# Two heads to a product in the weighted values, and the second layer in one block

## The chip, the cores and the metric

The kernel runs on one core of a Trainium2 chip. A core has five engines that run their own instruction streams: TensorE (PE; its weight loads are listed apart as PEld), VectorE (DVE), ScalarE (ACT), GpSimd (POOL) and SyncE (SP), which issues most transfers. They are kept in order by semaphores. Matmul results land in PSUM, from which DVE and ACT read them. The metric is the device time of one execution in microseconds, the median of several runs. Everything is float32.

## The reference

Two layers on an image batch of 16 x 192 channels x 56 x 56. The first is a shifted-window attention block with six heads of 32 channels and windows of 7 x 7 = 49 positions; the second scales a masked 3 x 3 depthwise convolution by weights made from the image's own mean. Cut to what matters (`_ln` normalises over channels; the roll by 3 and the split into windows are left in words):

```python
h = roll(_ln(x), -3); win = windows_of_7x7(h)            # (-1, 49, 192)
q, k, v = split_heads(win @ qkv_w + qkv_b)                # 6 heads of 32
attn = softmax((q * SCALE) @ k.T + rel_bias + mask)
out = (attn @ v) @ proj_w + proj_b
x1 = x + roll(windows_back(out), 3)
y = gelu(_ln(x1) @ fc1_w + fc1_b) @ fc2_w + fc2_b
x2 = x1 + y
# second layer: weights from the image's mean, then four causal taps
t = relu(bn(mean(x2) @ w1.T)); wt = (t @ w2.T + b2) * mask
out = depthwise_conv3x3(x2, wt) + bias
```

## The kernel before

The work is cut into 64 strips (`S = 16 * NU`, NU = 4). A strip is seven rows of the image's upper half and seven of its lower half; the halves lie in partitions 0 to 63 and 64 to 127 (index `ab`), channels in three groups of 64 (`g`). So a strip holds 2 x 8 windows of 49 positions, `UT = 392` columns for each half.

A software pipeline runs over rounds `r` (the loop at L1349): round r computes the scores of strip r, the weighted values and the projection of strip r-1, the first layer (192 to 768 channels, six chunks `f`) of strip r-2 and the second layer (768 to 192) of strip r-3, and queries, keys and normalisation of strips ahead. Rounds 3 to 63 are full ones.

Nothing is issued straight away. `add(engine, duration, fn, reads, writes)` enters an operation into a plan with the author's estimate of its duration; `Plan.order()` (L72) then lists all of it. TensorE keeps the order in which its operations were added. The other engines take, among operations that are ready soonest, the one that is due first. The resulting list is one program: each engine executes its instructions strictly in that order, waiting on semaphores where the framework finds that two instructions touch the same data.

PSUM is four buffers `ps0` to `ps3` of 128 x 2 x 512 numbers, taken in turn by `bank()` (L186). A buffer has two halves, `p[:, 0]` and `p[:, 1]`, with a key of their own in the plan.

The steps that matter:

- `queries_keys` (L465): three products; q goes by ACT to `q128` and `q2` as one run of 392 columns (with 16 columns of padding), k by DVE and ACT to block tables `kbd`, `kbd2` (L492, L514, L523).
- `scores` (L533): 3 x 16 products, each 64 queries (49 and the 15 columns after them) against the keys of two heads, 98 columns. Then for each of three buffers on DVE the position bias is added (L574) and the maximum taken (L584), POOL subtracts it (L589), ACT exponentiates (L596), DVE sums and inverts (L601, L602), POOL scales (L607).
- `turn_shares` (L611): DVE transposes the shares in blocks of 32 x 32 (L618), and ten transfers on SP (L624) bring them to `pt` with keys in the partitions, queries in two blocks of 32 and 17.
- `values` (L642): v of strip r, into `v0` or `v1` by ACT (L665).
- `weighted` (L672): 4 window pairs x 2 halves x 6 heads x 2 windows = 96 products, each 32 channels of one head by 64 query columns (L690). Four ACT copies (L714) bring the result to `o1` (four heads) and `o2` (two heads), stored with the seven window rows outermost.
- `projection` (L717): `narrow` for o2 (L726), then `broad` for o1 (L740); DVE adds the result to the strip (L764).
- `first_layer` (L770): products (L777) and the ACT gelu into `hid` (L789). `second_layer` (L795): for each g, six steps f of two products (L816), then DVE adds the result to the strip (L803). Each g takes a PSUM buffer of its own, of which it uses half 0.
- `deviations` and `spread` (L306, L347): TensorE folds sums over channels (L316), ACT and DVE make the variance `m2` (L330, L337), ACT makes 1/sqrt with Ln and Exp (L352, L359), and transfers spread it over the partitions as `rb`.
- `taps` and `conv` (L831, L886): the second layer of the network, on TensorE for one small product per image (L846), then ACT and DVE, which apply four taps (L907, L931).

`second_layer` and `weighted` are generators before. The round lets them alternate on TensorE: three steps f after the scores, then one window pair and two steps f in turn, three more steps, then v, the projection, and the last six steps. The first layer is split after two chunks to let `deviations` in.

Of the kernel before, what the change touches and what calls it, by code (L numbers as in the profile page):

```python
# [33 lines left out]
TL = 32  # L34

# [105 lines left out]
def tile_swin_then_dynamic_conv(  # L141
# [64 lines left out]
    q128 = sb("q128", 128, 2, UP)  # L206
    q2 = sb("q2", 128, UP)
# [6 lines left out]
    o1 = sb("o1", 128, WS, 2, NWIN, WS)  # L214
    o2 = sb("o2", 128, WS, 2, NWIN // 2, WS)
# [17 lines left out]
    bnr = sb("bnr", 128, 4, RED)  # L233
# [14 lines left out]
    full = sb("full", 128, 128)  # L248
    eps_t = sb("eps", 128, 1)
    zero = sb("zero", 128, IMG)  # L250
    ident = sb("ident", 64, 64)
# [54 lines left out]
    def deviations(norms, later=False):  # L306
# [36 lines left out]
        if later:  # L343
            return
        spread(norms)

    def spread(norms):  # L347
        lanes = slice(64 * norms[0], 64 * norms[-1] + 64)
# [32 lines left out]
    def first_deviations():  # L381
# [9 lines left out]
        add("PE", 1.4, product, [("f", 0, 0), ("f", 0, 1), "blk"], [pk])  # L391
# [73 lines left out]
    def queries_keys(s, parts):  # L465
        d = xs1
        for i in parts:
# [15 lines left out]
            if i == 0:  # L483
                def go(p=p):
                    nc.scalar.activation(
                        q128[:, :, 0:UT], p[:, :, 0:UT], AF.Identity, bias=qbs[:, 0:1], scale=SCALE
                    )
                add("ACT", 0.95, go, [pk, "qb"], ["q128"])
# [12 lines left out]
            else:  # L501
                for ab in range(2):
                    def go(p=p, ab=ab):
                        nc.scalar.activation(
                            q2[P(ab), 0:UT],
                            p[0:64, ab, 0:UT],
                            AF.Identity,
                            bias=qbs[0:64, 1:2],
                            scale=SCALE,
                        )  # L510
                    add("ACT", 0.62, go, [pk, "qb"], [("q2", ab)])
# [21 lines left out]
    def scores(s):  # L533

        last = s % NU == NU - 1
        for j in range(3):
            p, pk = bank()

            def product(j=j, p=p):
                for w in range(NWIN):  # L540
                    for i in range(2):
                        cols = slice(w * N, w * N + 64)
                        if j < 2:
                            a, k = q128[P(i), j, cols], kbd[P(i), j, w]
                        else:
                            a, k = q2[P(i), cols], kbd2[P(i), w]
# [3 lines left out]
                            a,  # L550
# [6 lines left out]
            if j < 2:  # L557
                keys = ["q128", ("kbd", 0), ("kbd", 1), "qpad"]
            else:
                keys = [("q2", 0), ("q2", 1), "qpad"]  # L560
                keys += [("kbd2", ab, h) for ab in range(2) for h in range(2)]
# [110 lines left out]
    def weighted(s):  # L672


        pa, ka = bank()
        pb, kb = bank()

        def product(pair):
            for ab in range(2):
                for h in range(HEADS):  # L680
                    for w in range(2):
                        if h < 4:
                            j, slot = ab, (h // 2) * 8 + pair * 2 + h % 2
                            at = (ab * 4 + pair) * 64
                            lane, p = TL * h, pa
                        else:
                            j, slot = 2, ab * 8 + pair * 2 + h - 4
                            at = (ab * 2 + pair % 2) * 64
                            lane, p = TL * (h - 4) + 64 * (pair // 2), pb
                        nc.tensor.matmul(  # L690
                            p[lane : lane + TL, w, at : at + 64],
                            v[s % 2][P(w), ab, pair, h * HD : (h + 1) * HD],
                            pt[P(w), :, 16 * j + slot, :],
# [5 lines left out]
        for pair in range(4):  # L699
            add(  # L700
                "PE",
                0.75,
                lambda pair=pair: product(pair),
                PTK() + [("v", s % 2, pair // 2), "ptz"],
                [ka, kb],
            )
            yield
        o1v = o1.rearrange("p r a (q w) c -> p w (a q) r c", w=2)
        o2v = o2.rearrange("p r a (q w) c -> p w (a q) r c", w=2)
        for o, p, k, n, dur in ((o1v, pa, ka, 8, 0.54), (o2v, pb, kb, 4, 0.37)):  # L710
            for w in range(2):
                def go(o=o, p=p, n=n, w=w):
                    src = p[:, w, 0 : 64 * n].rearrange("p (q t) -> p q t", t=64)[:, :, 0:N]
                    nc.scalar.copy(o[:, w], src.rearrange("p q (r c) -> p q r c", c=WS))  # L714
                add("ACT", dur, go, [k], [("o", n, w)])

    def projection(s):  # L717
        pf, kf = bank()
        pq, kq = bank()
        keys = [("o", n, w) for n in (4, 8) for w in range(2)]  # L720

        def narrow():
            for m in range(G):
                for ab in range(2):
                    for i, p in ((0, pf), (1, pq)):
# [3 lines left out]
                            o2[P(i), :, ab],  # L729
                            start=(m % 2 == 0),  # L730
                            stop=False,
# [4 lines left out]
        def broad():  # L736
            for i, p in ((0, pf), (1, pq)):
                for m in range(G):
                    for ab in range(2):
# [3 lines left out]
                            o1[:, :, ab, 4 * i : 4 * i + 4],  # L743
                            start=False,
                            stop=True,
# [4 lines left out]
        add("PE", 1.05, narrow, keys + ["wp"], [kf, kq])  # L750
        add("PE", 2.0, broad, keys + ["wp"], [kf, kq])
# [18 lines left out]
    def first_layer(s, chunks):  # L770
        for f in chunks:
# [23 lines left out]
    def second_layer(s):  # L795

        b, u = divmod(s, NU)
        xv = rows(s).rearrange("p g r c -> p g (r c)")
        for g in range(G):
# [205 lines left out]
    def masks():  # L1005
# [5 lines left out]
        def go():  # L1011
            nc.gpsimd.memset(q128[:, :, UT:UP], 0.0)
            nc.gpsimd.memset(q2[:, UT:UP], 0.0)
# [510 lines left out]
```

## Time and profile before

| what | value |
|---|---|
| median of 3 runs | 2927.38 us (2925.48 to 2928.41) |
| the profiled execution | 2926.42 us, span 2924.6 us, mean granted TensorE clock 0.988 |
| busy, share of the span | PE 97%, DVE 60%, POOL 56%, ACT 48% |
| TensorE groups, busy | L816 837.8, L777 786.5, L473 404.9, L653 266.3, L690 190.4, L548 147.0 us |
| one steady round (scores to scores, 1647.80 to 1691.47) | 43.67 us, TensorE busy 43.67, clock 1.00 |

Busy times of groups on one engine can overlap at their ends, since matmuls are pipelined; the distance from the start of one block to the start of the next is what a block costs. In a timeline line the first number is the start, the second the length, both in us, then engine, line, operation, output and input, and the number of instructions merged. Each float32 product is two instructions. What stands in brackets is idle time before and what ended it. A share of busy time says nothing of what a wait costs; for that one looks at what TensorE waits for.

### The profile page before, as it was taken

The numbers are of one execution on the slowest core, as the hardware profiler recorded it, in microseconds if no ns is written. First come the engines' busy times: TensorE is split into PE (matmuls) and PEld (weight loads), VectorE is DVE, ScalarE is ACT, GpSimd is POOL, SyncE is SP. The second block draws the span as 40 slices with busy tenths as digits, with TensorE's granted clock in tenths as the row PEclk, the third lists the DMA queues.
The fourth block names the chain that finished last, engine by engine and source line by source line (L and its number), as shares of the span: only waits on it lengthen the run. The fifth ranks groups of instructions, "written<-read, shape, count | busy, mean of one in ns | idle before, by whom it ended". The sixth has DMA issues, their size and how long they took to land.

```text
span 2924.6 us, 90872 instructions
## 1 busy us (share of the span) xinstructions
PE 2849.4 (97%) x40401; PEld 1702.8 (58%) x40401; DVE 1758.0 (60%) x2873; ACT 1407.2 (48%) x1890; POOL 1641.6 (56%) x1424
## 2 busy tenths in 40 slices
PE   6799999999999999999999999999999999999996
PEld 4565565565565565565565565565655555565552
DVE  4644664846657475674846657575674846657554
ACT  2344454545445454454545455454454555455443
POOL 4554664755656565664755656565664755656530
PEclk8899999999999999999999999999999999999998
DMA  3511141323314223141322414223141322413221
GB/s 88 109 43 41 42 109 34 82 60 67 87 31 95 59 60 76 42 105 38 82 60 66 88 31 94 59 60 76 42 104 39 81 61 66 88 31 73 47 46 48
DMA packets 123715, 190.84 MB, mean 65 GB/s; under 512 B 31693, under 2 KB 98106, under 8 KB 123322
## 3 DMA queue, kind: packets, MB, share of 16 engines
q1 hardware_dynamic: 118954, 185.01, 28.7%
q8 instruction: 317, 5.19, 0.7%
q10 hardware_dynamic: 4368, 0.02, 0.1%
q14 instruction: 76, 0.62, 0.1%
HBM read 67.57 MB, written 38.93 MB: 36 GB/s over the span
## 4 chain that ended last, share of the span: by engine, by line
PE 95%; DVE 1%; POOL 1%; issue 1%; ACT 1%; DMA 0%; ACTq 0%; DVEq 0%; SPq 0%; POOLq 0%
PE ps L816 28%; PE ps L777 26%; PE ps L473 13%; PE ps L653 8%; PE ps L690 6%; PE ps L740 5%; PE ps L548 5%; PE ps L726 2%; PE ps L316 2%; DVE hid L931 0%; PE ps L846 0%; POOL xs L429 0%; DMA wqkv<-in_L_conv_qkv_w_dram 0%; DVE bt L1250 0%; POOL fold L302 0%
## 5 line engine op out<-in xcount | busy, mean ns | idle before, releaser
L816 PE MATMUL ps<-hid,wf 128*64 128x392 f32 x4608 | 837.8, 499 | 0.3 <-issue 0.3
L777 PE MATMUL ps<-xs,wf 64*128 64x392 f32 x4608 | 786.5, 492 | 0.0
L589 POOL TENSOR_TENSOR e<-e,top 128x784 f32<-128x784 f32 x192 | 314.1, 1659 | 603.0 <-DVE top L584 603.0
L777 PEld LDWEIGHTS ps<-xs,wf 64*128 64x128 f32 x4608 | 440.4, 187 | 315.8 <-issue 16.2
L816 PEld LDWEIGHTS ps<-hid,wf 128*64 128x64 f32 x4608 | 303.5, 136 | 323.2 <-issue 289.6
L789 ACT ACTIVATE hid<-ps,b1f 128x784 f32<-128x784 f32 x384 | 345.8, 913 | 259.3 <-PE ps L777 254.7
L931 DVE SCALAR_TENSOR_TENSOR y<-x,wt,y 128x770 f32<-128x770 f32 x270 | 389.5, 1453 | 64.7 <-ACT y L907 61.0
L473 PE MATMUL ps<-xs,wqkv 64*128 64x392 f32 x2304 | 404.9, 503 | 19.0 <-POOL xs L440 19.0
L607 POOL TENSOR_TENSOR e<-e,tot 128x784 f32<-128x784 f32 x192 | 316.8, 1664 | 43.3 <-DVE tot L602 27.4
L473 PEld LDWEIGHTS ps<-xs,wqkv 64*128 64x128 f32 x2304 | 221.5, 190 | 201.2 <-POOL xs L440 29.8
L293 ACT ACTIVATE sq<-x 128x1176 f32<-128x1176 f32 x128 | 151.4, 1183 | 327.8 <-DVE x L764 235.5
L574 DVE TENSOR_TENSOR e<-ps,bt 128x784 f32<-128x784 f32 x192 | 175.0, 967 | 218.9 <-ACT hid L789 218.8
L300 POOL TENSOR_TENSOR fold<-sq 128x392 f32<-128x392 f32 x128 | 130.7, 1021 | 304.4 <-PE ps L316 268.5
L653 PE MATMUL ps<-wqkv,xs 64*64 64x192 f32 x6144 | 266.3, 326 | 0.0
L653 PEld LDWEIGHTS ps<-wqkv,xs 64*64 64x64 f32 x6144 | 231.0, 134 | 50.7 <-issue 36.1
L596 ACT ACTIVATE e<-e 128x784 f32<-128x784 f32 x192 | 165.2, 861 | 193.7 <-POOL e L589 193.4
L803 DVE SCALAR_TENSOR_TENSOR x<-ps,vecs,x 128x392 f32<-128x392 f32 x192 | 119.8, 624 | 227.1 <-PE ps L816 216.2
L429 POOL TENSOR_TENSOR xs<-x,rb 128x343 f32<-128x343 f32 x192 | 216.3, 1154 | 64.0 <-PE ps L653 61.5
L618 DVE STREAM_TRANSPOSE tt<-e 128x512 f32<-128x512 f32 x384 | 247.9, 687 | 3.4 <-POOL e L607 1.8
L690 PEld LDWEIGHTS ps<-pt,v 64*32 64x32 f32 x12288 | 149.7, 105 | 154.3 <-issue 117.0
L300 POOL TENSOR_TENSOR fold<-x 128x392 f32<-128x392 f32 x128 | 151.4, 1183 | 156.4 <-PE ps L316 124.4
L492 DVE TENSOR_SCALAR kbd<-ps,bq,mask 128x784 f32<-128x784 f32 x128 | 134.1, 1089 | 167.1 <-PE ps L473 167.1
(104 smaller groups left out, 3068.6 us busy)
## 6 DMA issues: line engine op xcount, KB each, us to landing
pt<-tt SPq DMA_DIRECT2D x256, 192.0 KB
x<-in_x_dram SPq DMA_DIRECT2D x112, 294.0 KB
out_dram<-y SPq DMA_DIRECT2D x135, 196.0 KB
pt<-tt SPq DMA_DIRECT2D x256, 96.0 KB
rb<-rsd SPq DMA_DIRECT2D x118, 196.0 KB
out_dram<-y SPq DMA_DIRECT2D x45, 154.0 KB
x<-in_x_dram SPq DMA_DIRECT2D x16, 168.0 KB
pt<-tt SPq DMA_DIRECT2D x128, 12.0 KB
```

Of the source, the lines that this page charges most:

```text
L300: nc.gpsimd.tensor_tensor(f, src[:, 0], src[:, 1], ALU.add)
L429: nc.gpsimd.tensor_tensor(d[:, g, 0 : nf * N].rearrange("p (w r c) -> p w r c", r=WS, c=WS), xv[:, g, :, cs].rearrange("p r (w c) -> p w r ...
L473: nc.tensor.matmul(p[:, ab, 0:UT], lhs_qk(ab, g, i), d[P(ab), g, 0:UT], start=(g == 0), stop=(g == G - 1), tile_position=(64 * ab, 0),)
L589: nc.gpsimd.tensor_tensor(ev, ev, top[j].broadcast_to([128, 16, N]), ALU.subtract)
L607: nc.gpsimd.tensor_tensor(ev, ev, tot[j].broadcast_to([128, 16, N]), ALU.mult)
L618: nc.vector.transpose(tt[:, kb, 16 * j : 16 * j + 16], src)
L653: nc.tensor.matmul(p[P(w % 2), ab, i * DIM : (i + 1) * DIM], d[P(ab), g, w * N : w * N + 64], wqkv[P(ab), g, 2 * DIM :], start=(g == 0), s ...
L690: nc.tensor.matmul(p[lane : lane + TL, w, at : at + 64], v[s % 2][P(w), ab, pair, h * HD : (h + 1) * HD], pt[P(w), :, 16 * j + slot, :], s ...
L777: nc.tensor.matmul(p[:, ab, 0:UT], wf1[P(ab), g, f * 128 : (f + 1) * 128], xs2[P(ab), g], start=(g == 0), stop=(g == G - 1), tile_position ...
L789: nc.scalar.activation(hid[:, f], p[:, :, 0:UT], AF.Gelu, bias=b1f[:, f : f + 1])
L816: nc.tensor.matmul(p[P(ab), 0, 0:UT], wf2[:, f, g * 64 : (g + 1) * 64], hid[:, f, ab], start=(f == 0), stop=(f == NFC - 1), tile_position= ...
L931: nc.vector.scalar_tensor_tensor(dst, s_, w[:, g, t : t + 1], dst, ALU.mult, ALU.add)
```

## The change

Line numbers shift by a few. What changes:

- Weighted values: two heads share a product. 64 channels (two heads of v) meet the shares of both heads, in 2 heads x 2 blocks x 25 columns = 100 columns; the blocks of head 0 with head 0 and head 1 with head 1 are what is wanted, the others are not read. 48 products in three PSUM buffers instead of 96 in two. Twelve copies of 32 partitions, six on ACT and six on DVE, take out the wanted blocks, instead of four on ACT.
- For that the 49 queries are stored as 25 and 24 in two blocks of 32, from q onwards: q is written in two parts, bias and mask tables follow suit (with four more transfers at the start). `o1` and `o2` are stored by window with 49 in a row, and the projection reads them in row order. `broad` comes before `narrow`.
- Order on TensorE in a full round: scores, v, weighted values, second layer whole, projection, q and k, first layer whole, deviations. Before: scores, second layer and weighted values in turns, v, projection, rest of the second layer, q and k, first layer with deviations inside.
- The second layer takes two PSUM buffers: g = 0 and 1 in the halves of one, g = 2 in the other.
- Tables that are used only at the start (`full`, `ident`, `bnr`) share space with `hid`.

```diff
-    q128 = sb("q128", 128, 2, UP)
-    q2 = sb("q2", 128, UP)
+    q128 = sb("q128", 128, 2, NWIN, 2, TL)
+    q2 = sb("q2", 128, NWIN, 2, TL)
...
-    o1 = sb("o1", 128, WS, 2, NWIN, WS)
-    o2 = sb("o2", 128, WS, 2, NWIN // 2, WS)
+    o1 = sb("o1", 128, 2, NWIN, N)
+    o2 = sb("o2", 128, 2, NWIN // 2, N)
...
             if i == 0:
-                def go(p=p):
-                    nc.scalar.activation(
-                        q128[:, :, 0:UT], p[:, :, 0:UT], AF.Identity, bias=qbs[:, 0:1], scale=SCALE
-                    )
-                add("ACT", 0.95, go, [pk, "qb"], ["q128"])
+                for h, lo, hi in ((0, 0, QL), (1, QL, N)):
+                    def go(p=p, h=h, lo=lo, hi=hi):
+                        nc.scalar.activation(
+                            q128[:, :, :, h, 0 : hi - lo],
+                            p[:, :, 0:UT].rearrange("p a (w t) -> p a w t", t=N)[:, :, :, lo:hi],
...
+                    add("ACT", 0.6, go, [pk, "qb", "qpad"], [("q128", h)])
...
     def weighted(s):
-        pa, ka = bank()
-        pb, kb = bank()
-        def product(pair):
-            for ab in range(2):
-                for h in range(HEADS):
+        banks = [bank() for _ in range(3)]
+        def product(j):
+            p = banks[j][0]
+            for t in range(4):
+                for h in range(2):
                     for w in range(2):
...
+                        shares = pt[P(w), :, slot : slot + 2, 0:QL]
                         nc.tensor.matmul(
-                            p[lane : lane + TL, w, at : at + 64],
-                            v[s % 2][P(w), ab, pair, h * HD : (h + 1) * HD],
-                            pt[P(w), :, 16 * j + slot, :],
+                            p[lane : lane + 64, w, t * 128 : t * 128 + 4 * QL],
+                            v[s % 2][P(w), ab, pair, head * HD : (head + 2) * HD],
+                            shares.rearrange("p q k c -> p k q c"),
...
+            for i in range(4):
+                lanes = slice(TL * i, TL * i + TL)
+                at = (i % 2) * 2 * QL
+                src = p[lanes].rearrange("p w (t c) -> p w t c", c=128)[:, :, :, at : at + N]
...
+                if i < 2:
+                    add("ACT", 0.6, lambda dst=dst, src=src: nc.scalar.copy(dst, src), [k], [("o", j, i)])
+                else:
+                    add("DVE", 0.56, lambda dst=dst, src=src: nc.vector.tensor_copy(dst, src), [k], [("o", j, i)])
...
-                            o1[:, :, ab, 4 * i : 4 * i + 4],
+                            o1[:, ab, 4 * i : 4 * i + 4].rearrange(by_rows, c=WS),
...
-        add("PE", 1.05, narrow, keys + ["wp"], [kf, kq])
-        add("PE", 2.0, broad, keys + ["wp"], [kf, kq])
+        add("PE", 2.05, broad, o1k + ["wp"], [kf, kq])
+        add("PE", 1.05, narrow, o2k + ["wp"], [kf, kq])
...
     def second_layer(s):
+        pairs = [bank(), bank()]
         for g in range(G):
-            p, pk = bank()
+            p, pk = pairs[g // 2][0][:, g % 2], pairs[g // 2][1][g % 2]
...
-            nc.gpsimd.memset(q128[:, :, UT:UP], 0.0)
-            nc.gpsimd.memset(q2[:, UT:UP], 0.0)
+            nc.gpsimd.memset(q128, 0.0)
+            nc.gpsimd.memset(q2, 0.0)
...
+        if has(r):
+            values(r, (0, 1))
+        if has(r + 1) and r > -2:
+            scaled1(r + 1)
...
-        for n in (2, 2, 2):
-            next(weighing, None)
-            few(n)
-        for _ in weighing:
-            pass
-        few(3)
+        if has(r - 1):
+            weighted(r - 1)
         if has(r):
             turn_shares()
+        if has(r - 3):
+            second_layer(r - 3)
...
             table("gelu_and_others")
-            first_layer(r - 2, (0, 1))
-            if norms:
-                deviations(norms, True)
-            first_layer(r - 2, range(2, NFC))
+            first_layer(r - 2)
             table("natural_log_exp_and_others")
-            if norms:
-                spread(norms)
-        elif norms and r > -2:
+        if norms and r > -2:
             deviations(norms)
```

## The prediction

> **What bounds the kernel now.** I read the page first: busy shares, then the chain that ended last.
>
> ```profile
> span 2924.6 us, 90872 instructions
> ...
> PE 2849.4 (97%) x40401; PEld 1702.8 (58%) x40401; DVE 1758.0 (60%) x2873; ACT 1407.2 (48%) x1890; POOL 1641.6 (56%) x1424
> ...
> PE 95%; DVE 1%; POOL 1%; issue 1%; ACT 1%; DMA 0%; ACTq 0%; DVEq 0%; SPq 0%; POOLq 0%
> ```
>
> TensorE is the path. TensorE's waits add up to some 47 us, nearly all in the first 130 us, so every microsecond of matmul time counts, and so does every new wait. Next, the timeline of TensorE over one steady round (scores to scores, 1647.80 to 1691.47, 43.67 us) and at the end of the run:
>
> ```profile
> 1647.80 2.25 PE L548 MATMUL ps<-kbd,q 64*64 64x98 f32 x96
> 1649.98 2.20 PE L816 MATMUL ps<-hid,wf 128*64 128x392 f32 x12
> 1652.11 0.72 PE L690 MATMUL ps<-pt,v 64*32 64x64 f32 x48
> 1652.76 1.54 PE L816 MATMUL ps<-hid,wf 128*64 128x392 f32 x8
> 1654.23 0.73 PE L690 MATMUL ps<-pt,v 64*32 64x64 f32 x48
> ...
> 1661.35 4.13 PE L653 MATMUL ps<-wqkv,xs 64*64 64x192 f32 x96
> 1665.30 1.18 PE L726 MATMUL ps<-o,wp 64*64 64x196 f32 x24
> ...
> 1668.45 4.12 PE L816 MATMUL ps<-hid,wf 128*64 128x392 f32 x24
> 1672.50 6.20 PE L473 MATMUL ps<-xs,wqkv 64*128 64x392 f32 x36
> ...
> 1682.57 0.87 PE L316 MATMUL ps<-fold,blk 128*32 128x196 f32 x16
> ```
>
> ```profile
> 2858.64 12.07 PE L816 MATMUL ps<-hid,wf 128*64 128x392 f32 x72
> 2870.64 12.12 PE L777 MATMUL ps<-xs,wf 64*128 64x392 f32 x72
> 2882.70 12.07 PE L816 MATMUL ps<-hid,wf 128*64 128x392 f32 x72
> ```
>
> I take a block's cost from start to next start. The reader is to see that the second layer (L816) is cut in six, and what it costs whole: 12.00 us.
>
> Last, the views of who waits for whom between the engines that read PSUM (ACT and DVE groups, and their timeline):
>
> ```profile
> 1546.92 0.68 ACT L514 ACTIVATE kbd<-ps,km,mask 64x392 f32<-64x392 f32 x1 [3.04 <-PE ps L473]
> ...
> 1547.64 1.30 DVE L523 TENSOR_SCALAR kbd<-ps,bq,mask 64x392 f32<-64x392 f32 x2 [0.59 <-ACT kbd L514]
> 1548.98 0.68 ACT L514 ACTIVATE kbd<-ps,km,mask 64x392 f32<-64x392 f32 x1 [1.37 <-DVE kbd L523]
> ```
>
> ACT reads half 0 of one PSUM buffer, DVE half 1, and still they take turns, with 0.04 us between: the program orders accesses by whole buffers of two halves. This carries the prediction.
>
> **What TensorE gains, per round.**
> - Second layer: its six blocks take 2.13+1.47+1.47+1.46+2.13+4.05 = 12.71 us; whole 12.00. Gain 0.71.
> - Weighted values: four visits of 0.65+0.66+0.70+0.70 = 2.71 us. After: 48 products of 64 by 64 with 100 columns, one block. The scores are the same thing with 98 columns (48 products, 2.18 us), so 2.18 x 100/98 = 2.22. Gain 0.49. Bounds: the rate of the v block (3.95 us for 192 columns) gives 2.06; adding 0.12 for a cut (12 records of L816 take 2.13 against 2.00 pro rata) gives 2.34. I stay with the scores, the nearest shape.
> - First layer uncut: 4.04+0.80+8.10 becomes 12.06+0.80. Gain 0.08.
> - Scores, v, projection and q/k keep their products (2.18, 3.95, 3.15, 6.03). The projection now reads o in runs of 7 numbers where it had 28; no row has such short runs. Bounds: 0 to a doubling of its 3.15 us; I take 0, as the runs of 32 in L690 kept up with 14 ns per record.
>
> New round without waits: 2.18+3.95+2.22+12.00+3.15+6.03+12.06+0.80 = 42.39, a gain of 1.28 us; 61 full rounds (r = 3 to 63): 78 us.
>
> A rule speaks against the weighted values. The Trainium skill, "TensorEngine Tiling (Array Packing)", Available Configurations: the array is 8 tiles at 64x32, 4 at 64x64. By it and the scores' rate (12 x 98 column steps in 2.18 us, 1.85 ns each), 12 x 64 steps cost 1.42 us now and 12 x 100 cost 2.22: a loss of 0.8 us a round, 49 us in all, where the trace's 2.71 gives a gain of 30. The trace decides.
>
> **What the change makes TensorE wait for.** Three pieces, read from the code and the instruction order of the changed program.
>
> (a) The second layer puts g=0 and g=1 in the two halves of one buffer. The changed program lets the third step (f=2) of g=1 wait for the DVE addition that ends g=0 (L803 before), which itself waits for steps f=0,1 of g=1. In every round this is a full turn TensorE-DVE-TensorE. Before, each g had its own buffer and L816 shows no such wait.
>
> (b) In DVE's queue that addition stands behind: three score additions, three maxima, six copies of weighted values, and the first sum of exponentials with its reciprocal. Before, there were no copies on DVE.
>
> (c) The copies of one buffer alternate DVE, ACT, DVE, ACT, each waiting for the one before, as L514/L523 do. ACT's three exponentials stand behind its six copies, and the first sum waits for the first of them.
>
> Clock from the start of the scores: DVE's additions start at 1.04 (1648.84 in the trace), last 2.66, maxima 2.71: free at 6.41 (6.77 with the m2 subtraction of 0.36 between). First weighted buffer: 2.18+3.95+0.74 = 6.87, and a reader starts 0.28 later (v: 1663.60 against 1663.32): 7.15. The copies: 6 on DVE and 4 on ACT lie in series (the last ACT copy of a buffer runs beside the next buffer's first DVE copy). ACT has a row, 392 elements from PSUM: 523 ns. DVE has none: 566 ns (L402, same size) is nearest; 409 ns (196 elements, L764) and 696 ns (L523) bound it. 6 x 0.56 + 4 x 0.52 + 8 x 0.04 = 5.76: until 12.91. First exponential 0.86+0.04: 13.81. Sum and reciprocal 0.04+0.94+0.25: 15.04. Addition 0.63: 15.67; TensorE goes on at 15.72 (0.05 after DVE, as at 2895.80).
> TensorE is ready for f=2 of g=1 at 2.18+3.95+2.22 + 16/36 x 12.00 = 13.68. **Wait: 2.04 us**, more than the 1.28 gained: 0.76 lost, x 61 = 46 us.
>
> Bounds of this wait: if DVE is on time, 0.21 (2894.91 against 2894.70) + 0.63 + 0.05 = 0.9; with 696 and 583 ns (L504) per copy the series is 6.8 and the wait 3.1. DVE's sums, transposes and additions behind it shift with TensorE, and nothing else is due earlier.
>
> The Trainium skill, "PSUM — Partial Sum Buffer", PSUM bank collisions, says that two engines may work at once on different banks, or in different 32-partition quadrants of one. By it neither (a) nor (c) need wait, and the sum would be 2926.4 - 78 + 13 = 2861. The rows of L514 and L523 show the program waiting nevertheless, and it is the program that runs.
>
> **The other edits.**
> - deviations after the first layer: the subtraction m2 (0.36) on DVE stands after the first score addition in the rounds with convolutions: 1.04+0.89+0.36+0.05 = 2.34, and v needs its buffer at 2.18. Wait 0.16 x 45 rounds = 7 us (0 to 0.5 each). rs leaves about 0.35 later, for a q/k product 20 us off: hidden.
> - q written in two blocks: ACT 2 x about 0.5 for 0.91, 4 x about 0.37 for 2 x 0.58: +0.4 us on ACT, 48% busy. First layer's fourth buffer needs them; in the walk they end 0.8 us ahead. Zero; if that cover went, at most 0.4 x 61 = 24.
> - Convolutions (1.45 each, four between g=1 and the projection's additions) end before q/k's third buffer, because TensorE comes 2 us later; without the wait of (a) they would cost about 0.6 in 45 rounds.
> - pt transfers: transposes end some 7 us before the next scores, ten issues take 7.4 us (1664.57), and the weighted values start 6.1 into the round against 4.3 before. Hidden.
> - Start: POOL's zeroing of q, 1536 elements at the 2.66 us of 3072, about 1.3 us, fits in its 2.27 us wait for x. Four more SP issues delay what follows them by 4 x 0.65 us; the bias tables on DVE start at 39.6, long after. kbd2 is now ahead of the tables (the 5.48 us wait goes; the next wait, on xs, shrinks by about 3). In r = 1 and 2 no second layer hides the copies: 5.76 in series plus two sums where 1.37 stood, about +7. Net +4 (-3 to +8).
> - End: two whole second layers with the turn of 0.9 each: +2.
>
> Sum against the profiled execution, 2926.42 us (span 2924.6 and 1.8 around it): +46 +7 +4 +2 = 2985.4; the median of the runs, 2927.38, lies 1.0 higher: **2986**.
>
> **Rivals.**
> 1. Faster: DVE reaches the addition nearly on time. One mechanism: the copies' series. If it takes under 4.8 us in place of 5.76, the wait of (a) is under 1.07 and the kernel wins (1.28 less the 13 us of the other edits over 61 rounds). For it: they touch 32 partitions and contiguous rows of 49. Against: L714 shows 365 ns for 196 elements and 523 for 392, so size along a partition sets it. At the floor of 0.9: 2926.4 - 0.38 x 61 + 13 = 2916, 2917 on the median. Chance 0.17, waits up to 1.16 counted in.
> 2. The turn of (a) costs nothing and the gain stands: 2927 - 78 + 13 = 2862. Against it: the wait is in the program, with 0.9 as its least price. 0.03.
> 3. Copies as slow as the upper rows: 3.1 per round, 2987 + 1.1 x 61 = 3053. For it: L523 on DVE. 0.08.
> 4. Short runs slow the projection: doubled, 2986 + 3.15 x 61 = 3178. 0.03.
>
> **Numbers.** The likeliest case (0.69) is a wait of 1.5 to 2.8: net 0.2 to 1.5 lost per round, with the 13 of the other edits 2953 to 3032, and 2986 in it. Reaching under the floor of rival 1, by the 2.06 us that the weighted values may take (0.16 x 61 = 10), and into rival 3: 2906 to 3040. Within 0.2% (5.9 us; less can't be told from no change in this kernel) means a wait of about 0.97 to 1.16 us: 0.07 of rival 1. Faster: its other 0.10 and 0.03 of rival 2. Slower: 0.69 + 0.08 + 0.03 = 0.80.
>
> **What would show it.** L816's line (L821 after) with a wait on DVE (L808) in nearly every round, some 2 us each, 100 to 130 us in all; otherwise dense TensorE. Weighted values as one block of 96 records in 2.2 us, the second layer in 12.0 plus the wait. DVE copies with ACT as releaser and ACT copies with DVE as releaser. Wrong if the wait is near 0.9, if the copies overlap, or if the projection's block leaves 3.15.

## The result, and the profile after

The changed kernel takes 3001.45 us (median of 4 runs, 2999.95 to 3006.45) against 2927.51 (4 runs, 2925.48 to 2928.41): 1.0257 times as long, 95% interval 1.0239 to 1.0274. The profiled execution took 2999.95 us, span 2998.2, granted clock 0.987 (0.988 before). The forecast was 2986 in 2906 to 3040, slower.

The page of the changed kernel, busy time by engine and the chain that ended last:

```profile
PE 2798.4 (93%) x34257; PEld 1713.7 (57%) x34257; DVE 1924.7 (64%) x3257; ACT 1510.7 (50%) x2210; POOL 1626.8 (54%) x1424
...
PE 75%; DVE 14%; ACT 6%; issue 3%; POOL 1%; DMA 0%; DVEq 0%; ACTq 0%; POOLq 0%
PE ps L782 25%; PE ps L821 15%; PE ps L468 13%; PE ps L653 8%; DVE o L718 7%; PE ps L745 5%; ACT o L716 3%; PE ps L731 3%; DVE tot L601 2%; PE ps L548 2%; ACT e L596 2%; PE ps L689 2%; PE ps L317 2%; DVE x L808 1%; DVE m L338 1%
```

TensorE works 51 us less than before and the kernel takes 73.6 us more of span. The chain, 95% TensorE before, now runs through DVE and ACT: copies (L718, L716), exponentials (L596), sums (L601), the addition (L808). What TensorE waits for (waits by releaser: total us, times, longest):

```profile
PE ps L821 <- DVE x L808: 110.9, 64, 2.3
PE ps L468 <- POOL xs L435: 17.7, 4, 6.3
PE ps L548 <- DVE m L338: 11.7, 15, 0.8
PE ps L745 <- ACT q L505: 11.3, 2, 5.8
```

One wait carries it: the second layer, on DVE's addition, once in every round. Here is a steady round on TensorE, 44.65 us where it was 43.67:

```profile
1643.94 2.25 PE L548 MATMUL ps<-kbd,q 64*64 64x98 f32 x96
1646.28 4.13 PE L653 MATMUL ps<-wqkv,xs 64*64 64x192 f32 x96
1650.23 2.24 PE L689 MATMUL ps<-pt,v 64*64 64x100 f32 x96
1652.40 5.49 PE L821 MATMUL ps<-hid,wf 128*64 128x392 f32 x32
1659.67 6.80 PE L821 MATMUL ps<-hid,wf 128*64 128x392 f32 x40 [1.79 <-DVE x L808]
1666.31 2.34 PE L745 MATMUL ps<-o,wp 128*64 128x196 f32 x24
1668.57 1.31 PE L731 MATMUL ps<-o,wp 64*64 64x196 f32 x24
1669.81 6.20 PE L468 MATMUL ps<-xs,wqkv 64*128 64x392 f32 x36
```

The second layer breaks off after 32 records: 24 of g = 0 and the first two steps of g = 1. And the same stretch on DVE:

```profile
1651.16 0.56 DVE L718 COPY o<-ps 32x392 f32<-32x392 f32 x1 [0.55 <-PE ps L689]
1652.27 1.17 DVE L718 COPY o<-ps 32x392 f32<-32x392 f32 x2 [0.55 <-ACT o L716]
1653.98 1.17 DVE L718 COPY o<-ps 32x392 f32<-32x392 f32 x2 [0.54 <-ACT o L716]
1655.69 0.57 DVE L718 COPY o<-ps 32x392 f32<-32x392 f32 x1 [0.55 <-ACT o L716]
1657.69 0.97 DVE L601 TENSOR_REDUCE tot<-e 128x16 f32<-128x784 f32 x1 [1.43 <-ACT e L596]
1658.70 0.25 DVE L602 RECIPROCAL tot<-tot 128x16 f32<-128x16 f32 x1
1658.98 0.63 DVE L808 SCALAR_TENSOR_TENSOR x<-ps,vecs,x 128x392 f32<-128x392 f32 x1
```

ACT in the same stretch, from its last copy on:

```profile
1656.30 0.48 ACT L716 COPY o<-ps 32x392 f32<-32x392 f32 x1 [0.64 <-DVE o L718]
1656.81 2.35 ACT L596 ACTIVATE e<-e 128x784 f32<-128x784 f32 x3
```

Between its copies DVE waits half a microsecond for ACT, then 1.43 for an exponential that ACT started 0.03 us after its own last copy, then sums; TensorE goes on 0.06 us after the addition. This is the predicted chain, link by link.

Adding the distances from block start to block start over the first 60 full rounds gives the account (us; the last column is experiment e10, told of below):

| block | before | after | difference | e10 |
|---|---|---|---|---|
| scores | 130.9 | 151.2 | +20.3 | 139.2 |
| v | 237.1 | 236.5 | -0.6 | 234.5 |
| weighted values | 164.4 | 132.4 | -32.0 | 136.3 |
| second layer | 762.3 | 835.6 | +73.3 | 714.2 |
| projection | 188.7 | 210.5 | +21.8 | 195.0 |
| q, k | 361.8 | 361.7 | -0.1 | 361.7 |
| first layer | 728.8 | 716.8 | -12.0 | 728.7 |
| deviations, taps | 60.0 | 60.0 | 0.0 | 60.0 |
| sum | 2634.0 | 2704.8 | +70.8 | 2569.6 |

The 70.8 us are nearly all of the 73.6; start, last full round and end hold the rest.

### The profile page after: what moved, and what is told of

It reads as the page before. It is cut to its first block, busy times and chain, and to the rows that moved or that the text cites. A ratio compares the mean times of both kernels' runs of the same rounds, so it can differ in the third digit from the quotient of the medians.

```text
span 2998.2 us, 79159 instructions
## 1 busy us (share of the span) xinstructions
PE 2798.4 (93%) x34257; PEld 1713.7 (57%) x34257; DVE 1924.7 (64%) x3257; ACT 1510.7 (50%) x2210; POOL 1626.8 (54%) x1424
## 4 chain that ended last, share of the span: by engine, by line
PE 75%; DVE 14%; ACT 6%; issue 3%; POOL 1%; DMA 0%; DVEq 0%; ACTq 0%; POOLq 0%
PE ps L782 25%; PE ps L821 15%; PE ps L468 13%; PE ps L653 8%; DVE o L718 7%; PE ps L745 5%; ACT o L716 3%; PE ps L731 3%; DVE tot L601 2%; PE ps L548 2%; ACT e L596 2%; PE ps L689 2%; PE ps L317 2%; DVE x L808 1%; DVE m L338 1%
## 5 line engine op out<-in xcount | busy, mean ns | idle before, releaser
L821 PE MATMUL ps<-hid,wf 128*64 128x392 f32 x4608 | 788.2, 496 | 110.9 <-DVE x L808 110.9
L589 POOL TENSOR_TENSOR e<-e,top 128x784 f32<-128x784 f32 x192 | 283.1, 1501 | 151.6 <-DVE top L584 151.6
L935 DVE SCALAR_TENSOR_TENSOR y<-x,wt,y 128x770 f32<-128x770 f32 x270 | 319.9, 1225 | 2.7 <-ACT y L911 2.7
L718 DVE COPY o<-ps 32x392 f32<-32x392 f32 x384 | 218.1, 568 | 140.3 <-ACT o L716 111.1
L481 ACT ACTIVATE q<-ps,qbs 128x400 f32<-128x400 f32 (+1 forms) x128 | 68.5, 589 | 408.5 <-PE ps L468 408.5
L716 ACT COPY o<-ps 32x392 f32<-32x392 f32 x384 | 184.8, 481 | 167.3 <-DVE o L718 156.0
L453 POOL TENSOR_TENSOR xs<-x,rb 128x392 f32<-128x392 f32 x192 | 254.1, 1350 | 24.4 <-PE ps L821 13.6
L301 POOL TENSOR_TENSOR fold<-x 128x392 f32<-128x392 f32 x128 | 131.3, 1025 | 246.9 <-PE ps L317 166.7
L601 DVE TENSOR_REDUCE tot<-e 128x16 f32<-128x784 f32 x192 | 182.2, 949 | 83.3 <-ACT e L596 83.3
L665 ACT COPY v<-ps 128x768 f32<-128x768 f32 x128 | 102.4, 800 | 181.7 <-PE ps L653 181.7
```

The source lines that it names most:

```text
L301: nc.gpsimd.tensor_tensor(f, src[:, 0], src[:, 1], ALU.add)
L589: nc.gpsimd.tensor_tensor(ev, ev, top[j].broadcast_to([128, 16, N]), ALU.subtract)
L716: add("ACT", 0.6, lambda dst=dst, src=src: nc.scalar.copy(dst, src), [k], [("o", j, i)])
L718: add("DVE", 0.56, lambda dst=dst, src=src: nc.vector.tensor_copy(dst, src), [k], [("o", j, i)])
L821: nc.tensor.matmul(p[P(ab), 0:UT], wf2[:, f, g * 64 : (g + 1) * 64], hid[:, f, ab], start=(f == 0), stop=(f == NFC - 1), tile_position=(0, ...
L935: nc.vector.scalar_tensor_tensor(dst, s_, w[:, g, t : t + 1], dst, ALU.mult, ALU.add)
```

## Experiments

**e1: g = 0 and g = 2 share the buffer, g = 1 has its own.** From the changed kernel:

```diff
-            p, pk = pairs[g // 2][0][:, g % 2], pairs[g // 2][1][g % 2]
+            p, pk = pairs[g % 2][0][:, g // 2], pairs[g % 2][1][g // 2]
```

> The second layer's g=0 and g=2 share a buffer and g=1 has its own; copies, products and the number of buffers (22 a round) stay. Theory (the shared buffer makes TensorE wait for g=0's addition while g=1 is already due): the wait of the second layer on DVE goes, since g=2 comes 4 us later; a steady round goes from 44.65 to 44.65 - 1.91 = 42.74 us; the time to 3000 - 1.91 x 61 - 2 x 0.8 = 2882 us (2872 to 2895), below the kernel before. DVE and ACT copies still take turns (idle of some 150 and 110 us). Rival (DVE is late as a whole, and whoever next needs one of its buffers pays): the wait shows up again at g=2, at the projection or at the q/k products, and the time stays above 2940.

Measured: 2883.46 us (2880.91 to 2884.56), 0.9852 of before (0.9837 to 0.9867). One index is worth 118 us. The second layer's line and the two copy lines of e1 (groups: busy, mean ns | idle before, and for what):

```profile
L821 PE MATMUL ps<-hid,wf 128*64 128x392 f32 x4608 | 772.5, 494 | 1.0 <-ACT o L716 1.0
...
L718 DVE COPY o<-ps 32x392 f32<-32x392 f32 x384 | 218.1, 568 | 139.9 <-ACT o L716 110.5 <-PE ps L689 25.5
L716 ACT COPY o<-ps 32x392 f32<-32x392 f32 x384 | 184.3, 480 | 167.3 <-DVE o L718 155.9
```

The copies wait for each other exactly as in the changed kernel (140.3 and 167.3 us there) and it no longer matters: the addition is wanted 4 us later. The second layer takes 11.90 us whole, so the shared buffer cost 13.91 - 11.90 = 2.01 us a round, 1.79 of it shown as idle; the rest is the break itself. The rival, that DVE is late as a whole and whoever needs it next pays, is refuted: of the 121.6 us that the second layer wins in 60 rounds, 6.4 come back in the first layer and 2.0 in the weighted values.

**e2: one engine for all four copies of a buffer.** Sharing of g = 0 and 1 kept:

```diff
-                if i < 2:
+                if j != 1:
                     add("ACT", 0.6, lambda dst=dst, src=src: nc.scalar.copy(dst, src), [k], [("o", j, i)])
```

> The sharing of g=0 and g=1 stays; the four copies of one weighted buffer are on one engine (ACT, DVE, ACT in place of two and two). With 4 copies in place of 6, DVE's addition now stands ahead of the first sum in its queue. Theory (the size of the wait is set by the copies' alternation and by what stands ahead of the addition): copies of two buffers run side by side, DVE is done with its four (4 x 0.57 us) some 2 us before the addition is due, and the wait falls to its floor of 0.8 to 0.9 as in the last rounds: 3000 - 61 x (1.91 - 0.85) = 2935 us (2925 to 2950). Rival 1 (the copies have nothing to do with it): unchanged, 3000. Rival 2 (sharing costs nothing once DVE is on time): 2882.

Measured: 2942.44 us (2940.93 to 2943.77), 1.0054 of before (1.004 to 1.0069). DVE of e2:

```profile
1660.21 2.29 DVE L718 COPY o<-ps 32x392 f32<-32x392 f32 x4 [1.24 <-PE ps L689]
1666.47 0.62 DVE L808 SCALAR_TENSOR_TENSOR x<-ps,vecs,x 128x392 f32<-128x392 f32 x1 [3.96 <-PE ps L821]
...
1667.02 0.96 DVE L601 TENSOR_REDUCE tot<-e 128x16 f32<-128x784 f32 x1
```

Here DVE waits 3.96 us for TensorE and the turn still costs TensorE 0.81 of idle time in a round, 1.03 with the break. That is the floor: half of the loss is the turn itself. (With the addition earlier in the program, TensorE now stops after 28 records of the second layer, one step before the 32 of the changed kernel, here and in e8.)

**e8: copies as in the change, the addition ahead of the first sum.** e2 changed the copies and, through the plan, also the place of the addition. This separates them:

```diff
-            add("ACT", 0.85, power, ["table"], [("e", j)])
+            add("ACT", 0.85, power, ["table"], [("e", j)], lag=1.2 if j == 0 else 0.0)
```

> The changed kernel with one planner delay (1.2 us behind the first exponential), which puts the second layer's addition of g=0 ahead of the first sum and reciprocal in DVE's queue; products, buffers and copies stay, and the copies still take turns. Theory (what makes the addition late is the 1.25 us of the first sum ahead of it, not the end of the copies, which is 12.3 us into the round where the addition is due at 13.9): the wait falls to its floor of 0.81, as in e2: 3001 - 60 x 0.98 = 2942 us (2932 to 2952). Rival (the copies' series itself is too late): the wait stays above 1.4 us, 2975 or more.

Measured: 2947.36 us (2943.85 to 2947.99), 1.0068 of before (1.0054 to 1.0082). DVE of e8:

```profile
1666.13 0.57 DVE L718 COPY o<-ps 32x392 f32<-32x392 f32 x1 [0.55 <-ACT o L716]
1667.75 0.63 DVE L808 SCALAR_TENSOR_TENSOR x<-ps,vecs,x 128x392 f32<-128x392 f32 x1 [1.04 <-PE ps L821]
```

The delay also moves some operations of ACT and POOL. The copies still take turns, yet DVE is through with them 1.04 us early, and the wait is 0.74 (0.96 with the break). So the other half of the loss is the sum and reciprocal (1.25 us) that the queue held ahead of the addition. The copies' series matters only because it delays the exponential for which that sum waits.

**e3: e1, and the weighted values stored with window rows outermost.** The projection reads runs of 28 numbers again:

```diff
-    o1 = sb("o1", 128, 2, NWIN, N)
+    o1 = sb("o1", 128, WS, 2, NWIN, WS)
...
-                            o1[:, ab, 4 * i : 4 * i + 4].rearrange(by_rows, c=WS),
+                            o1[:, :, ab, 4 * i : 4 * i + 4],
```

> As e1, and the weighted values are stored with the window rows outermost again, so that the projection reads runs of 28 numbers; its products and their order (broad, then narrow) stay as in the changed kernel, the copies write runs of 7. If the runs of 7 made the projection go from 3.15 to 3.50 us: its block is 3.15 again and the time is that of e1 less 0.35 x 62 = 22 us, 2860. If the new order of broad and narrow did it: 3.50, and the time of e1. The copies may be longer for their runs of 7; nothing waits for them by then.

Measured: 2873.0 us (2871.74 to 2874.53), 0.9818 of before (0.9803 to 0.9832). The projection on TensorE's timeline, up to the start of q and k, in e1:

```profile
1688.98 2.34 PE L745 MATMUL ps<-o,wp 128*64 128x196 f32 x24
1691.24 1.31 PE L731 MATMUL ps<-o,wp 64*64 64x196 f32 x24
1692.49 6.20 PE L468 MATMUL ps<-xs,wqkv 64*128 64x392 f32 x36
```

and in e3:

```profile
1682.76 2.16 PE L745 MATMUL ps<-o,wp 128*64 128x196 f32 x24
1684.85 1.23 PE L731 MATMUL ps<-o,wp 64*64 64x196 f32 x24
1686.00 6.20 PE L468 MATMUL ps<-xs,wqkv 64*128 64x392 f32 x36
```

From 1688.98 to 1692.49 is 3.51 us, from 1682.76 to 1686.00 3.24: runs of 7 cost TensorE 0.27 us a round, 15.8 us in 60 rounds (210.6 to 194.8). Of the time, 10.5 came through; in the rounds after the taps the first layer's waits on the queries' copies (7.7 us in all, 1.9 in e1) ate part of it. 0.10 of the growth from 3.15 remains.

**e6: e3 with `narrow` first, and the deviations within the first layer again.** Both as in the kernel before.

> As e3, with the narrow products of the projection ahead of the broad ones again, and the deviations again within the first layer (after its second block). Each shows in its own block of a round. Scores: the 0.16 and 0.81 us waits on m2 go, 2.52 mean to 2.18, -20 us in 60 rounds. Projection: if the order of broad and narrow made the rest of the growth (3.25 against 3.15), 3.15 and -6 us; if not, 3.25. First layer: two cuts as before, 11.95 to 12.15, +12; its waits on the queries' copies (7.7 us) may go. Sum 2873 - 20 - 6 + 12 - 8 = 2851 (2843 to 2868), 2.6% under the kernel before.

Measured: 2876.22 us (2873.11 to 2881.68), 0.9833 (0.9819 to 0.9846): no gain over e3, a miss. The scores' waits did go (2.07 us in all rounds), but the first layer's cuts cost the expected 0.2 a round, its waits on the queries' copies stayed (6.8 us), and the end grew by 9 us, 7 of them deviations that wait for POOL's sums. The projection took 3.30: the order of its two parts isn't the remaining 0.10. Since the second layer grew by 0.10 at the same time (11.90 to 12.00 with `narrow` behind it), what moves about looks like the price of one change of tile shape between blocks; that is argued from block lengths, not isolated.

**e10: e3, with m2 ahead of the first score addition on DVE.** One planner duration of the square (`0.4` to `0.3`); TensorE's and ACT's orders are the same.

> As e3, with one planner duration changed (0.3 in place of 0.4 us for the square of the means), which only moves the subtraction m2 ahead of the first score addition in DVE's queue. In e3 the square ends at 1619.73 and the scores' first block can be read at 1620.28, so the 0.35 us of m2 fit in DVE's idle time before it. The scores' block goes to 2.18 us in all rounds, from 2.34 and, in the 15 rounds after the taps, 3.11: 45 x 0.16 + 15 x 0.9 = 20 us; 2873 - 20 = 2853 (2846 to 2864). Rival (another wait stands behind it): 2870 or more.

Measured: 2863.39 us (2858.01 to 2866.06), 0.9786 of before (0.9773 to 0.98), the fastest kernel here. The scores take 2.07 us in 45 rounds instead of 2.34. In the 15 rounds after the taps m2 already stood ahead of the additions, behind small DVE operations of the taps (L861 to L863); there it kept its place, and TensorE its 0.81 us wait. So half of the expected 20 us came. DVE of e10:

```profile
242.07 0.36 DVE L338 TENSOR_TENSOR m<-ps,m 128x196 f32<-128x196 f32 x1 [8.87 <-ACT m L331]
242.51 2.73 DVE L574 TENSOR_TENSOR e<-ps,bt 128x784 f32<-128x784 f32 x3
```

**e4: single heads, 50 columns, in one row.** What is the pairing worth by itself? From e3: 96 products of one head, with the change's blocks of 25 (50 columns in place of 64), four ACT copies; each g has a buffer.

```diff
-                            p[lane : lane + 64, w, t * 128 : t * 128 + 4 * QL],
-                            v[s % 2][P(w), ab, pair, head * HD : (head + 2) * HD],
-                            shares.rearrange("p q k c -> p k q c"),
+                                p[lane : lane + TL, w, at : at + 2 * QL],
+                                v[s % 2][P(w), ab, pair, h * HD : (h + 1) * HD],
+                                pt[P(w), :, 16 * j + slot, 0:QL],
```

> As e3, but the weighted values are 96 products of one head each (64 by 32 stationary, 50 columns, in one row) with four ACT copies of 128 partitions, as before, instead of 48 products of two heads (64 by 64, 100 columns) with twelve copies; the second layer has a buffer for each g. Theory A (time goes by columns, four products at a time, whatever their width): 2.71 x 50 / 64 = 2.12 us in place of 2.17, so the pairing gains nothing beside what leaving out the empty columns gains; total as e3, 2850 to 2862. Theory B (each matmul record takes 14 ns at least, as before): 2.7 us, 2860 + 0.53 x 62 = 2893. Theory C (the rule of eight tiles at 64 by 32): 1.1 us, 2860 - 1.06 x 62 = 2794.

Measured: 3024.39 us (3022.18 to 3032.88), 1.0332 of before (1.0315 to 1.0349). No theory had this. Its waits by releaser have a line that no other kernel had at this size:

```profile
PE ps L689 <- issue: 112.4, 54, 3.3
```

TensorE's timeline in three rounds one after another:

```profile
378.34 1.59 PE L689 MATMUL ps<-pt,v 64*32 64x50 f32 x147
382.16 0.67 PE L689 MATMUL ps<-pt,v 64*32 64x50 f32 x45 [2.23 <-issue]
...
423.08 1.69 PE L689 MATMUL ps<-pt,v 64*32 64x50 f32 x156
427.53 0.58 PE L689 MATMUL ps<-pt,v 64*32 64x50 f32 x36 [2.76 <-issue]
...
470.05 1.95 PE L689 MATMUL ps<-pt,v 64*32 64x50 f32 x164
475.31 0.46 PE L689 MATMUL ps<-pt,v 64*32 64x50 f32 x28 [3.31 <-issue]
```

"issue" means that TensorE waited for nothing that the profile shows. The break is at record 147, 156, 164: it wanders by 8 or 9 a round. The second layer behind it also slows: 762.7 us in 60 rounds against 714.2 in e3, with only 4.5 us of idle shown. That is the granted clock. In 28 of the 60 rounds it falls to half for 3.4 us (once 6.8), during a stall of 1.84 to 3.32 us or up to 1.5 us after it; e3 has no such stretch in these rounds. Half of that time, where it overlaps the second layer, makes 43.4 of the 48.5 us. Two stretches of 3.5 us at the start of the second layer, after the first and the third of the stalls above (the x after PE counts matmuls; the number after the last bracket is the clock):

```profile
382.80:386.30 3.50, 3.50 (x23) 1.59 (x24) 1.22 (x2) 3.48 (x7) 0.20 (x1) 1.00 0.02 5
475.80:479.30 3.50, 3.50 (x12) 1.29 (x14) 1.22 (x2) 3.48 (x7) 0.00 (x0) 0.52 0.02 5
```

Not every stall is followed by one. Where no break falls into the block, the weighted values take 1.96 us, less than the pairs' 2.17.

**e9: pairs, but each product in two halves of 50 columns.** From e3, the 64 by 64 tiles kept, twice the records:

```diff
+                        for k2 in range(2):
+                            to = t * 128 + 2 * QL * k2
...
-                            shares.rearrange("p q k c -> p k q c"),
+                                shares[:, :, k2],
```

> As e3, but each of the 48 products of 100 columns is given as two products of 50 columns with the same stationary 64 by 64: the same columns and the same result, twice the records (192), no 64 by 32 tile. It tells apart what stalled TensorE in e4 and, less, in e5. If it is the number of short records in a row (384 again with the scores and v): stalls without a releaser of 60 us or more in the weighted values, and a time near e4's 3024, at least 2940. If it is the 64 by 32 shape: no such stalls and 2873 to 2885, a little more for the products' own rate.

Measured: 3021.38 us (3018.22 to 3027.06), 1.0331 (1.0317 to 1.0345). From its waits:

```profile
PE ps L691 <- issue: 68.6, 50, 2.7
```

and on its timeline a round without a break:

```profile
755.93 3.09 PE L691 MATMUL ps<-pt,v 64*64 64x50 f32 x192
758.95 6.47 PE L823 MATMUL ps<-hid,wf 128*64 128x392 f32 x38
```

The stalls come back without any 64 by 32 tile. Order, tiles and columns are those of e3; only the number of records in the row has grown, from 288 to 384 with scores and v. Beside that, 96 products of 50 columns take 3.02 us in 64 by 64 tiles and 1.96 in 64 by 32, so some 51 of the 148 us over e3 are this slower rate (0.85 a round).

**e5 and e7: long matmuls between the short ones.** e5 is e4 with g = 0 of the second layer between v and the weighted values; e7 adds the edits of e6.

```diff
+        second = second_layer(r - 3) if has(r - 3) else iter(())
+        next(second, None)
         if has(r - 1):
             weighted(r - 1)
```

> As e4 (single heads, 50 columns), but the second layer's g=0 stands between v and the weighted values; nothing else. In e4, 384 short matmul records in a row (scores, v, weighted values) were followed or broken by stalls that no semaphore explains (112 us over 54 rounds, at a place that moves by some 8 records from round to round). Theory (the supply of instructions falls behind in a row of short matmuls; long ones let it catch up): the 24 long records in between take the stalls away: 3024 - 109 (weighted values) - 45 (second layer, 762.7 against 714 us in e3) + 7 (one more cut) = 2875 us (2860 to 2892), and the weighted values take 1.96 + 0.12 us. Rival (the stall belongs to the 64 by 32 products themselves): it stays with them, above 2980.

> As e5, with the two edits of e6. If the theory of e5 holds: 2875 - 14 = 2861 or, with 2.08 in place of 2.17 us for the weighted values, 2855 (2843 to 2875), level with e6: the pairing of the heads as such brings nothing that 50 columns a head don't bring. If the stalls stay: above 2960.

Measured: e5 2957.01 us (2952.25 to 2959.65), 1.0102 (1.0088 to 1.0116); e7 2951.8 (2949.09 to 2959.05), 1.009 (1.0076 to 1.0103). Both missed. The line of waits of e5:

```profile
PE ps L689 <- issue: 66.7, 22, 5.8
```

Fewer stalls, 22 for 54, but longer ones (57.1 us in 25 in e7); for six rounds and more there is none, and a round takes 42.1 to 43.2 us, then they come back. Four microseconds of long matmuls aren't enough. Each row of short records is now 192 long, less than the 288 that run almost freely in e3, so the length of a row alone doesn't decide.

**e11: the old order with 50 columns.** The kernel before's order, tiles, copies and buffers, with the queries in blocks of 25 and 24 as the only thing of the change that matters to TensorE.

> The kernel before's own order (second layer in six pieces, four visits of the weighted values between them, v afterwards, a buffer for each g, single heads in 64 by 32 tiles, four copies on ACT) with one thing of the change: queries in blocks of 25 and 24, so that a single-head product has 50 columns in place of 64. Of the change's two gains on TensorE, this one is then alone. If the visits follow the columns: e4's undisturbed block of 1.96 us in four visits of 0.49 with four cuts of 0.10 to 0.12, 2.40 us in place of 2.71, and 2925.4 - 0.31 x 61 = 2907 us (2900 to 2914). If a visit can't fall under 14 ns a record: 2925. Stalls without a releaser: at most some 5 us, since no row of short records is longer than 144. If the old order and 50 columns already give what the pairing was for: below 2870.

Measured: 2917.42 us (2915.36 to 2920.03), 0.9967 of before (0.9954 to 0.9979). That is above the stated range: the four visits take 2.48 us together (2.71 before; 2.40 expected), one stall costs 3.6 us with the half clock after it, and in 14 rounds after the taps the first layer waits for the queries' copies (5.1 us), as the kernel before does not. TensorE's timeline:

```profile
1646.35 0.68 PE L694 MATMUL ps<-pt,v 64*32 64x50 f32 x48
1646.96 1.54 PE L821 MATMUL ps<-hid,wf 128*64 128x392 f32 x8
1648.43 0.68 PE L694 MATMUL ps<-pt,v 64*32 64x50 f32 x48
```


Its waits have one line for the stalls on the weighted values:

```profile
PE ps L694 <- issue: 1.9, 2, 1.6
```

It has as many records of the same kinds as e4. On TensorE only the order differs (that of the projection's parts and of the deviations too), and the 112 us of stalls are gone.

## Why the prediction was right, point by point

- **The wait of (a).** Predicted 2.04 us a round, measured 1.79 idle and 2.01 with the break; 110.9 us in all where 100 to 130 was said. e1 shows that the shared buffer is the cause, since moving g = 1 out takes all of it.
- **Its size, (b) and (c).** The clock from the start of the scores held: copies from 7.22 to 12.84, when ACT's last one ends (predicted 7.15 to 12.91; a DVE copy is 0.57 as taken, an ACT copy 0.48 for 0.52), sum from 13.75 (13.85), addition from 15.04 as predicted, TensorE on at 15.73 (15.72). What the text left open is the share of each: e2 and e8 put about one microsecond on the turn and one on the sum ahead of the addition. The floor, 0.9, measured 0.74 to 0.81 idle, 0.96 to 1.03 with the break.
- **TensorE's gains.** 1.28 us predicted; weighted values 2.71 to 2.17 (2.22 said), second layer 12.70 to 11.90 without its wait (12.00 said), first layer 12.15 to 11.95: 1.54. The size is a fifth over the forecast, but the text read the weighted values' part as the pairing's, and e4 and e11 show otherwise: a single head's product is cheaper still (1.96 us) once its empty columns are gone and nothing cuts the block.
- **The rule weighed there.** The Trainium skill, "TensorEngine Tiling (Array Packing)", Available Configurations, has eight tiles at 64x32 for four at 64x64. The prediction set it aside for the trace's 2.71 us. e9 against e4 shows its direction: 3.02 to 1.96 us for the same columns and products, 1.5 times as fast, not twice.
- **m2, 7 us.** The 0.16 in 45 rounds came as predicted (2.34 for 2.18), though not as a plain wait: without it e10 has 2.07, so m2 costs 0.27 and the new order gives 0.11 back. Missed: in the 15 rounds after the taps the buffers are shifted by one, the third block of the scores meets m2, and waits 0.81 (11.7 us in all). Scores cost 20.3 us, not 7.
- **The projection, taken at 0.** This is the step that failed: "as the runs of 32 in L690 kept up" was no row for runs of 7. It grew by 0.36 us a round, 21.8 us, inside the stated bounds, and so one of the prediction's own signs of being wrong came true: the projection's block left 3.15. e3 gives 0.27 of it to the runs; 0.10 stays open.
- **Start, +4.** The first full round began at 154.75, 0.6 us earlier than before (155.31): the projection's two waits in rounds 1 and 2 came (5.8 and 5.4 us, against 2.7 and 3.3 before), and more was won elsewhere.
- **The sum.** In a steady round 0.98 us was lost (0.76 and 0.16 predicted). The 15 us between 2986 and 3001.45 are the projection (21.8) and the rounds after the taps (13), less the larger gain on TensorE (0.26 a round, 16) and the start (4.6). So the forecast is right for its main term by its mechanism, and its nearness to the total is in part luck: misses of 35 and of 21 us in opposite directions leave 15.
- **The queries' copies, taken at 0.** Held in the changed kernel, which has no wait of the first layer on them. The cover goes when the wait of (a) does: 1.9 us in e1, 7.7 in e3.
- **Rival 1, faster.** It needed the copies' series under 4.8 us; it took 5.62. And its price was wrong: it put the kernel at 2917 at the floor, but e2 and e8 reach the floor and take 2942 and 2947, still slower than before, since the projection (21.8) and the rounds after the taps (13) eat what the shorter wait leaves. So this way to a faster kernel wasn't open.
- **The PSUM rule weighed.** By it (the Trainium skill, "PSUM — Partial Sum Buffer", PSUM bank collisions: two engines may work at once on different banks or quadrants) nothing had to wait, and the prediction priced that at 2861. No run tests it: in every kernel here the program orders these accesses. e10, with the edits of e1 and e3 in it, comes to 2863 with that order kept and the one wait that mattered moved out of the way; DVE's and ACT's copies from different quadrants still wait for each other there (117.2 and 155.8 us). That 2863 and 2861 lie so near is chance.

## What to carry to other kernels

When accumulators share a PSUM buffer, pair those that lie farthest apart in time, not neighbours: the same two buffers cost 118 us in one assignment and nothing in the other. A reader that an in-order queue holds behind unrelated work is as late as that work, so look at what stands ahead of it, and move that, before making the work itself faster. And before gathering short matmuls into one row, count the records: here a cut cost TensorE about a tenth of a microsecond (first layer 12.15 us with two cuts, 11.95 whole), a row that was too long two or three, and the half clock behind it up to 1.7 more.

## What the runs showed of the hardware

- TensorE can stall without any releaser when many short matmul records follow each other. 288 records in a row (scores, v, pairs; 8.5 us) cost 1.9 us in a whole run of e3, 384 cost 68.6 and 112.4 us in e9 and e4, and as many records in pieces of at most 144 cost 1.9 in e11.
- What ends these stalls can be read from the packed traces, which keep the time of every packet of the queue that the profile lists as "instruction" (16,384 bytes each; in e4 a median of 258 TensorE instructions, matmuls and weight loads, start between one packet and the next). Of the stalls over 0.4 us in the weighted values, all 49 in e4, 47 in e9, 22 in e5 and 24 in e7 end 1.16 to 1.71 us after such a packet does; the waits of the scores on m2, which have a semaphore, lie anywhere from 0 to 17 us behind one. So TensorE stands there because its next instructions have not arrived; that is read from the timing, no run changes the supply itself.
- In no run do two of these packets start less than 3.2 us apart. An estimate from these numbers: 258 instructions in 3.2 us are 12.4 ns each. e4's weighted values use one every 5.1 ns (384 in 1.96 us), e9's every 7.9, the pairs every 11.3 (192 in 2.17 us). The place of the break wanders by a nearly constant step, as the edge of a block of fixed size would. The amount in all is not it: before and e11 move the same 317 packets as e4 (e3 269) and hardly stall. What would bring a packet sooner stays open, and so does what lets e5 go for rounds without a stall.
- A stall (1.62 us in e11, 1.84 to 3.32 in e4) can be followed by 3.4 us at half the granted clock: 28 times in e4's 60 rounds, some 50 us in all, 43.4 of them in the second layer.
- So what the pairing bought was records rather than columns: the 96 records fewer in the row are most of what e3 (2873 us) has over e4 (3024), by the stalls (112.4) and the half clock (some 50), less the 13 by which single heads' products are faster in themselves.
- A moving operand read in runs of 7 float32 numbers made 48 records of 196 columns take 3.51 us, 8% more than the 3.24 with runs of 28.
